# Seven block products of 256 columns in place of eight for two gates of a recurrent layer, in a fused graph stack on one core

## The chip, the cores and the metric

The kernel runs on one core of a Trainium2 chip, all in fp32. The metric is device microseconds of one execution; quoted times are medians of several executions. Engines are named as in the profile: PE (TensorE, with PEld for its weight loads), DVE (VectorE), ACT (ScalarE), POOL (GpSimd), SP (SyncE).

## The reference, cut to what matters

Four graph layers run over 128 graphs of 64 nodes with 256 features. Three are attention and relation layers, the fourth is a gated recurrence with three inner layers, and it is where the change is:

```python
def _gru_cell(inp, h, w_ih, w_hh, b_ih, b_hh):
    gi = inp @ w_ih.T + b_ih
    gh = h @ w_hh.T + b_hh
    i_r, i_z, i_n = jnp.split(gi, 3, axis=-1)
    h_r, h_z, h_n = jnp.split(gh, 3, axis=-1)
    r = jax.nn.sigmoid(i_r + h_r)
    z = jax.nn.sigmoid(i_z + h_z)
    n = jnp.tanh(i_n + r * h_n)
    return (1.0 - z) * n + z * h
...
for i in range(L):                                   # L = 3
    m = jnp.einsum('bnd,de->bne', h, weight[i])
    aggr = jnp.einsum('bst,bsd->btd', A, m)
    h = _gru_cell(aggr, h, w_ih, w_hh, b_ih, b_hh)
```

## The kernel before

16 groups of 512 rows pass through all layers. A plan interleaves the four layers of several groups on PE, so that while the recurrence of one group waits, attention matmuls of later groups fill in. The state is held transposed: `hT` and the aggregated `aT` have the 256 features in two blocks of 128 partitions and the 512 rows as columns. A "chunk" is 128 output features. For each chunk a gate of r or z is four matmuls of 512 columns (two feature blocks of `hT`, two of `aT`) into one PSUM bank:

```python
        class Gate:
            def __init__(self, name, chunk, n):
                self.pg = psum.tile([P, T], F32, name=name)          # one bank; "rz" has two, "nn" has two
            def add(self, w, m, k):
                nc.tensor.matmul(self.pg, w[:, k, self.chunk * P : (self.chunk + 1) * P], m[:, k, :], ...)

        def update(c, pr, ph, pi, pz, hT, hnew):
            nc.scalar.activation(r, pr, AF.Tanh, bias=brz[:, c : c + 1], scale=0.5)
            nc.scalar.activation(t, ph, AF.Identity, bias=bh[:, 4 + c : 5 + c])
            nc.vector.scalar_tensor_tensor(t, r, 1.0, t, op0=ALU.add, op1=ALU.mult)
            nc.vector.tensor_tensor(t, t, pi, ALU.add)
            nc.scalar.activation(nt, t, AF.Tanh, bias=bi[:, 4 + c : 5 + c])
            nc.gpsimd.tensor_tensor(d, hT[:, c, :], nt, ALU.subtract)
            yield
            nc.scalar.activation(z, pz, AF.Tanh, bias=brz[:, 2 + c : 3 + c], scale=0.5)
            nc.vector.scalar_tensor_tensor(d, z, 1.0, d, op0=ALU.add, op1=ALU.mult)
            nc.vector.scalar_tensor_tensor(hnew[:, c, :], d, 0.5, nt, op0=ALU.mult, op1=ALU.add)
        ... (allocations of the work tiles r, t, nt, z, d, two buffers each, cut)
```

`along` aggregates over the graph (matmul, then a copy of the bank into `aT`), `back` transposes the new state (PE, then a copy into `hnat`); both copies are on DVE. The eight PSUM banks are two each for "mm" and "tp" (the other layers and the helpers), "rz" and "nn".

## Time and profile before

| | before |
|---|---|
| median of 4 runs | 1657.4 us (1655.9 to 1661.9) |
| profiled span, mean granted clock of PE | 1654.2 us, 0.991 |
| PE / DVE / ACT / POOL busy | 95 / 61 / 28 / 17% |
| a steady group of 512 rows | 98.8 us |

The busy shares say which engine to look at first. The lines behind them, and PE's waits, stand in the prediction. One more reading: I split PE's time by the trace's starts of matmuls. Each record has a nominal spacing: the measured 429 ns at 512 and 216 ns at 256 columns with the line between them, and never under the 109 ns measured at 128 columns. Where a start is later than that, the doubling of a spacing in a stretch at half clock is counted as half clock, and the rest as a wait. Before, the spacings sum to 1537 us, half clock adds 7, waits are 87, and 23 us lie before the first and after the last matmul: 1654.

### The profile page before, as it was taken

How to read it: one execution, taken by the hardware profiler on the slowest of the kernel's cores; microseconds unless marked ns; L12 is line 12 of the kernel's file. 1: busy time of each engine (PE TensorE's matmuls, PEld its weight loads, DVE VectorE, ACT ScalarE, POOL GpSimd, SP SyncE). 2: the span in 40 equal slices, each digit the busy share in tenths (PEclk: the TensorE clock that was granted, in tenths of full speed). 3: DMA queues.
4: the chain of work that ended last, by engine and by line, in shares of the span. 5: the costliest groups of instructions: out<-in, count | busy, mean ns of one | idle time of the engine just before them, and what ended most of it. 6: DMA issues, size and time to landing. Idle time of an engine off the chain costs nothing.

```text
span 1654.2 us, 16189 instructions
## 1 busy us (share of the span) xinstructions
PE 1574.5 (95%) x5685; PEld 889.4 (54%) x5685; DVE 1014.3 (61%) x2403; ACT 470.9 (28%) x909; POOL 276.6 (17%) x252
## 2 busy tenths in 40 slices
PE   6898999999999999999999999999999999999997
PEld 4554555555555555556555555555555555554543
DVE  6777675757567475765757567475665656463533
ACT  3332332222222322323232232223222222222221
POOL 2111030211211111221211112111221111110110
PEclk9899999999999999999999999999999999999999
DMA  7000000100001000000100001010000000000000
GB/s 195 22 0 17 23 26 4 45 4 20 26 5 44 4 20 26 23 26 4 46 4 20 26 20 29 4 42 1 16 13 4 27 4 14 13 4 13 0 13 15
DMA packets 45890, 35.63 MB, mean 22 GB/s; under 512 B 21736, under 2 KB 44008, under 8 KB 45800
## 3 DMA queue, kind: packets, MB, share of 16 engines
q1 hardware_dynamic: 45240, 33.98, 7.3%
q8 instruction: 47, 0.77, 0.2%
q10 hardware_dynamic: 560, 0.52, 0.1%
q14 instruction: 43, 0.35, 0.1%
HBM read 25.96 MB, written 8.53 MB: 21 GB/s over the span
## 4 chain that ended last, share of the span: by engine, by line
PE 77%; DVE 14%; POOL 3%; issue 2%; ACT 2%; DMA 2%; SPq 0%; ACTq 0%; DVEq 0%; POOLq 0%
PE rz L295 33%; PE nn L295 16%; PE mm L627 6%; PE mm L231 6%; PE mm L250 4%; PE tp L264 3%; PE tp L166 3%; DVE hn L158 2%; PE tp L306 2%; DVE st L149 2%; PE mm L639 2%; DVE eb L568 1%; POOL xg L210 1%; POOL rstd L154 1%; DVE hn L209 1%
## 5 line engine op out<-in xcount | busy, mean ns | idle before, releaser
L295 PE MATMUL rz<-aT,wc 128*128 128x512 f32 x768 | 389.7, 599 | 6.7 <-DVE aT L268 6.7
L295 PE MATMUL rz<-hT,whh 128*128 128x512 f32 x768 | 386.9, 594 | 0.8 <-ACT r L317 0.8
L325 POOL TENSOR_TENSOR d<-hT,nt 128x512 f32<-128x512 f32 x96 | 124.0, 1292 | 831.6 <-ACT nt L323 824.6
L295 PEld LDWEIGHTS rz<-aT,wc 128*128 128x128 f32 x768 | 140.2, 190 | 161.2 <-issue 135.8
L295 PEld LDWEIGHTS rz<-hT,whh 128*128 128x128 f32 x768 | 135.8, 190 | 100.8 <-issue 95.1
L295 PE MATMUL nn<-aT,wc 128*128 128x512 f32 x384 | 189.4, 594 | 0.1
L295 PE MATMUL nn<-hT,whh 128*128 128x512 f32 x384 | 189.2, 593 | 0.0
L329 DVE SCALAR_TENSOR_TENSOR d<-z,d 128x512 f32<-128x512 f32 x96 | 66.1, 688 | 119.5 <-ACT z L328 68.4
L158 DVE TENSOR_SCALAR hn<-xg,mv,rstd 128x256 f32<-128x256 f32 x256 | 103.1, 447 | 43.3 <-POOL rstd L154 43.1
L149 DVE BATCH_NORM_STATS2 st<-xg 128x6 f32<-128x256 f32 x256 | 98.9, 403 | 47.3 <-POOL xg L210 41.3
L264 PEld LDWEIGHTS tp<-abd,hnat 128*128 128x128 f32 x768 | 100.4, 194 | 40.1 <-issue 30.0
L627 PE MATMUL mm<-wl,hT 128*128 128x512 f32 x248 | 119.8, 608 | 0.4 <-ACT hT L167 0.4
L317 ACT ACTIVATE r<-rz,brz 128x512 f32<-128x512 f32 x96 | 65.8, 686 | 187.9 <-PE rz L295 187.7
L166 PE MATMUL tp<-ident,hn 128*128 128x128 f32 x512 | 73.5, 281 | 45.3 <-DVE hn L158 27.4
L250 PEld LDWEIGHTS mm<-wh,eb 128*128 128x128 f32 x620 | 86.3, 191 | 55.8 <-issue 33.2
L295 PEld LDWEIGHTS nn<-aT,wc 128*128 128x128 f32 x384 | 70.9, 190 | 76.7 <-issue 72.7
L319 ACT ACTIVATE t<-nn,bh 128x512 f32<-128x512 f32 x96 | 65.8, 686 | 154.7 <-PE nn L295 154.7
L323 ACT ACTIVATE nt<-t,bi 128x512 f32<-128x512 f32 x96 | 69.2, 720 | 140.6 <-DVE t L321 102.8
L250 PE MATMUL mm<-wh,eb 128*128 128x65 f32 x620 | 100.5, 293 | 8.2 <-DVE eb L568 6.1
L328 ACT ACTIVATE z<-rz,brz 128x512 f32<-128x512 f32 x96 | 65.8, 685 | 147.7 <-PE rz L295 147.7
L264 PE MATMUL tp<-abd,hnat 128*128 128x128 f32 x768 | 102.2, 278 | 3.3 <-DVE fT L553 2.6
L166 PEld LDWEIGHTS tp<-ident,hn 128*128 128x128 f32 x512 | 60.6, 144 | 80.7 <-DVE hn L158 30.7
(161 smaller groups left out, 1822.6 us busy)
## 6 DMA issues: line engine op xcount, KB each, us to landing
out_dram<-hnat SPq DMA_DIRECT2D x16, 512.0 KB
xg<-in_x_dram SPq DMA_DIRECT2D x15, 512.0 KB
hT<-row SPq DMA_DIRECT2D x28, 256.0 KB
at<-in_adj_dram SPq DMA_DIRECT2D x64, 32.0 KB
ag<-in_adj_dram SPq DMA_DIRECT2D x16, 128.0 KB
t<-row SPq DMA_DIRECT2D x28, 64.0 KB
ihn<-in_L_gnn_w_ih_dram SPq DMA_DIRECT2D x1, 768.0 KB
hhn<-in_L_gnn_w_hh_dram SPq DMA_DIRECT2D x1, 768.0 KB
```

Of the source, the lines that this page charges most:

```text
L149: nc.vector.bn_stats(st[:, p, :], src[:, p, :])
L158: nc.vector.tensor_scalar(hn[:, p, :], src[:, p, :], mv[:, p, 0:1], rstd[:, p : p + 1], op0=ALU.subtract, op1=ALU.mult,)
L166: nc.tensor.transpose(pt[:, p * P : (p + 1) * P], hn[:, p, k * P : (k + 1) * P], ident)
L231: nc.tensor.matmul(pm[:, : D + 2 * heads], hT[:, k, p * P : (p + 1) * P], we[:, k, :], start=(k == 0), stop=(k == K - 1),)
L250: nc.tensor.matmul(pv[:, h, :], lhsT(p, h), wv[:, p, h, :], start=True, stop=True)
L264: nc.tensor.matmul(pa[:, p * P : (p + 1) * P], hnat[:, p, c * P : (c + 1) * P], abd[:, p, :], start=True, stop=True,)
L295: nc.tensor.matmul(self.pg, w[:, k, self.chunk * P : (self.chunk + 1) * P], m[:, k, :], start=(self.done == 0), stop=(self.done == self.n ...
L317: nc.scalar.activation(r, pr, AF.Tanh, bias=brz[:, c : c + 1], scale=0.5)
L323: nc.scalar.activation(nt, t, AF.Tanh, bias=bi[:, 4 + c : 5 + c])
L325: nc.gpsimd.tensor_tensor(d, hT[:, c, :], nt, ALU.subtract)
L329: nc.vector.scalar_tensor_tensor(d, z, 1.0, d, op0=ALU.add, op1=ALU.mult)
L627: nc.tensor.matmul(pm, hT[:, k, p * P : (p + 1) * P], wl[:, k, :], start=(k == 0), stop=(k == K - 1))
```

## The change

The intent: a product of a 2x2 block matrix of weights (gates r and z by two feature blocks) with a 2x2 block matrix of states (feature blocks by two halves of the rows) takes seven block products in place of eight, with sums of weights (made once), sums of states (per layer, POOL), and sums of products. Some of the latter are made by accumulating in PSUM, the others by ACT copying a running sum out of the bank and DVE adding it later. Bank "ry" takes M1, M6, M5, M3 one after the other.

```diff
+    def state_sums(m, ms, k):
+        if k == 0:
+            nc.gpsimd.tensor_tensor(ms[:, 0], m[:, 0, S1], m[:, 0, S0], ALU.subtract)
+        else:
+            nc.gpsimd.tensor_tensor(ms[:, 2], m[:, 1, S1], m[:, 0, S1], ALU.subtract)
+            nc.gpsimd.tensor_tensor(ms[:, 1], m[:, 1, S1], ms[:, 0], ALU.subtract)
+            nc.gpsimd.tensor_tensor(ms[:, 3], m[:, 1, S0], ms[:, 1], ALU.subtract)
     def recurrence(work, psum, start, src, abd, store):
         hT, aT = start
+        hS = work.tile([P, 4, T // 2], F32, name="hS")
+        aS = work.tile([P, 4, T // 2], F32, name="aS")
+        for k in range(K):
+            state_sums(hT, hS, k)
+            state_sums(aT, aS, k)
 ... (along, back: nc.vector.tensor_copy -> nc.scalar.copy for aT and hnat)
+            def mul(self, name, q, source):
+                lhsT, rhs = {
+                    1: (w[:, 0, cs], m[:, 0, S0]),
+                    2: (w[:, 1, cs], m[:, 1, S0]),
+                    3: (ws[:, 2, cs], m[:, 1, S1]),
+                    4: (w[:, 1, zs], ms[:, 3]),
+                    5: (ws[:, 0, cs], ms[:, 0]),
+                    6: (ws[:, 1, cs], ms[:, 1]),
+                    7: (w[:, 0, zs], ms[:, 2]),
+                }[q]
+                nc.tensor.matmul(ps[:, S0], lhsT, rhs, ...)
+            def r_there(self, h):
+                if h == S0:
+                    nc.vector.tensor_tensor(r, self.banks["rm"][:, S0], r, ALU.add)
+                    y = r
+                else:
+                    y = self.banks["ry"][:, S0]
+                nc.scalar.activation(r, y, AF.Tanh, bias=brz[:, self.c : self.c + 1], scale=0.5)
+                nc.vector.scalar_tensor_tensor(t, r, 1.0, t, op0=ALU.add, op1=ALU.mult)
+            def n_there(self, h):
+                nc.vector.tensor_tensor(t, t, self.banks["ni"][:, h], ALU.add)
+                nc.scalar.activation(t, t, AF.Tanh, bias=bi[:, 4 + self.c : 5 + self.c])
+                nc.gpsimd.tensor_tensor(self.d[:, h], self.hT[:, self.c, h], t, ALU.subtract)
+            def m1_there(self):   nc.scalar.copy(self.r[:, S0], self.banks["ry"][:, S0])
+            def m16_there(self):  nc.scalar.copy(self.z[:, S0], self.banks["ry"][:, S0])
+            def m165_there(self): nc.scalar.copy(self.z[:, S1], self.banks["ry"][:, S0])
+            def z_there(self, h):
+                nc.vector.tensor_tensor(z, self.banks["rz"][:, S0], z, ALU.add)
+                nc.scalar.activation(z, z, AF.Tanh, bias=brz[:, 2 + self.c : 3 + self.c], scale=0.5)
 ... (h_there: the two last steps by halves; the order of products in a layer; weight_sums)
-            turn = itertools.cycle(("mm", "tp", "rz", "nn"))
+            turn = itertools.cycle(("mt", "ry", "rm", "mt", "rz", "nh", "mt", "ni"))
-                return banks.tile(shape, dtype, name=name, tag=next(self.turn) if self.early else name)
+                tag = next(self.turn) if self.early else "mt" if name in ("mm", "tp") else name
+                return banks.tile(shape, dtype, name=name, tag=tag, bufs=3 if tag == "mt" else 1)
-                               {"hT": 3, "hnat": 2, "aT": 2, "r": 2, "t": 2, "nt": 2, "z": 2, "d": 2}))
+                               {"hT": 3, "hnat": 2, "aT": 2}))
-        start, period = 93.0, 93.0
+        start, period = 93.0, 88.0
 ... (two more numbers of the plan: 93.5 -> 88.5, 68 -> 65, recurrence work 68 -> 63)
```

S0 and S1 are the two halves of the 512 rows, and M1 to M7 the seven products, numbered in `mul`. "mm" and "tp" now share three banks; "ry", "rm", "rz", "nh" and "ni" have one each. The work tiles r, t, z, d and the new hS and aS have one buffer each. Some tiles of the preparation were also put into buffers of other tiles to make room; that is not shown here.

## The prediction

> **What bounds the kernel now.** I read the profile in this order: the page's busy shares and slices, the chain that ended last, the costliest groups, PE's waits in the middle of the run, the engines' busy time over whole groups, and two stretches of PE's order of time.
>
> ```profile
> PE 1574.5 (95%) x5685; PEld 889.4 (54%) x5685; DVE 1014.3 (61%) x2403; ACT 470.9 (28%) x909; POOL 276.6 (17%) x252
> ...
> PE   6898999999999999999999999999999999999997
> ...
> PE 77%; DVE 14%; POOL 3%; issue 2%; ACT 2%; DMA 2%; SPq 0%; ACTq 0%; DVEq 0%; POOLq 0%
> ...
> L295 PE MATMUL rz<-aT,wc 128*128 128x512 f32 x768 | 389.7, 599 | 6.7 <-DVE aT L268 6.7
> L295 PE MATMUL rz<-hT,whh 128*128 128x512 f32 x768 | 386.9, 594 | 0.8 <-ACT r L317 0.8
> ```
>
> PE is busy in nine tenths or more of almost every slice, and the matmuls that the change cuts (tile rz, gates r and z) are the costliest two groups. "Busy" alone could hide slack, since ends of matmuls are modelled, so I looked at whole groups (between stores of the output, at 1011.8, 1111.1, 1210.3 and 1308.2 us) and at what PE waits for between 190 and 1400 us:
>
> ```profile
> 1011.80:1111.10 99.30, 96.13 (x350) 53.98 (x349) 62.99 (x145) 27.89 (x53) 16.68 (x14) 1.00 0.07 19
> 1111.10:1210.30 99.20, 96.11 (x350) 54.01 (x349) 59.41 (x143) 28.35 (x53) 16.75 (x14) 1.00 0.06 18
> ```
>
> ```profile
> PE tp L166 <- DVE hnat L308: 14.3, 9, 2.1
> PE mm L250 <- DVE eb L568: 5.8, 7, 1.5
> PE rz L295 <- DVE aT L268: 5.0, 9, 0.9
> ```
>
> A group of 512 rows takes some 98.8 us, PE is idle under 3 us of it, and in 1210 us PE waits some 33 us in all. The matmuls of one group, counted at their spacing below, add up to about 98 us. So time removed from PE shows one for one, as long as no wait replaces it. The spacing is what counts, not the 594 ns of one record, which overlaps its neighbour:
>
> ```profile
> 1588.70 1.88 PE L295 MATMUL nn<-hT,whh 128*128 128x512 f32 x4
> 1590.41 1.88 PE L295 MATMUL nn<-aT,wc 128*128 128x512 f32 x4
> 1592.13 0.60 PE L306 MATMUL tp<-ident,hT 128*128 128x128 f32 x4
> ...
> 62.49 1.03 PE L609 MATMUL mm<-ihT,gT 128*128 128x256 f32 x4
> 63.36 0.49 PE L539 MATMUL mm<-dg1e,same 128*128 128x128 f32 x2
> ```
>
> Eight records of 512 columns take 3.43 us, 0.429 us each; four of 256 columns take 0.87 us, 0.217 us each. One fp32 matmul of the program is two records.
>
> **What the Trainium skill says.** "TensorE: Matmul & The Clock Gate", Back-to-back issue gap, gives N/2.4 + 2.5 ns per matmul, 216 ns at 512 columns; the trace shows twice that for each record in fp32, so the measurement is used. Its section on LDWEIGHTS gives P/1.2, 107 ns for 128 columns: eight attention records with 65 columns are spaced 0.105 us, which agrees, and a weight load therefore still fits behind a 256-column record of 0.217 us. "PSUM — Partial Sum Buffer", PSUM bank collisions raise a hardware error, says that two engines must not be in one bank at once: PE must wait until ACT or DVE has read a bank. Before, with two banks per kind, that wait is nearly absent (0.8 us on r). "SBUF — State Buffer", Who interferes with whom, says that a DVE instruction with two SBUF inputs and a POOL instruction that reads SBUF block each other. The trace is mixed: d<-z,d (two SBUF inputs) takes 688 ns and t<-t,nn (one from PSUM) 685 ns, but of two equal 1024-column steps one takes 1221 and the other 1424 ns.
>
> **The change part by part.**
> *PE.* 16 groups x 3 layers x 2 chunks = 96 chunks. Removed: 1536 records x 0.429 = 659 us. Added: 14 products x 2 records x 96 = 2688 x 0.217 = 583 us (577 if the half were exact). Saved: 76 to 82, say 78 us. In a steady group that is 4.9 of 98.8 us. Gate n, the aggregations and the layers before keep their matmuls.
> *DVE.* It loses the copies of aT (66.0) and hnat (43.8 us). Its four 512-wide steps a chunk (66.1 + 66.0 + 65.9 + 65.8 = 264 us) become eight 256-wide ones and three sums out of PSUM are added: 11 x 96 at 0.42 us (the o<-mm,rec row of 256 columns has 423 ns) = 444 us. Net +70: 1084 us, some 68% of the new time.
> *ACT.* It loses r, nt, z (65.8 + 69.2 + 65.8 = 201 us); gains six half-wide tanh (ACT's hT groups, 594 ns at 512 and 382 ns at 256 columns, give 0.83 ns a column, so 686 becomes 0.473 us, an estimate) x 96 x 0.473 = 272, three copies of 256 x 96 x 0.37 (the wh copies have 370 ns) = 107, and the aT and hnat copies, 160 x 0.583 (the wc copy of 512) = 93. Net +271: 742 us, 46%.
> *POOL.* The sums of states: eight a layer, 48 layers, 384 instructions of 256 columns. From 1292 ns at 512 and 2387 ns at 1024 columns the line gives 0.74 us at 256, an estimate: 284 us. The d steps halve and double, 192 x 0.74 = 142 instead of 124. With 16 weight sums (12 us, before the recurrence): about 590 us, 37%.
> No engine but PE comes near its limit. All three still deliver in order, and PE depends on them more: in the built program PE's waits on ACT go from 409 to 661, on DVE from 645 to 749, on POOL from 33 to 228.
> *What lands on the path.* The bank ry takes the products M1, M6, M5, M3 one after the other and ACT must copy the running sum out between them. After the last column of a product ACT starts some 0.3 us later (1642.9 to 1643.17 us for the last z), copies in 0.37, and the release costs about 0.1: 0.75 us, against 0.86 us of another product or gate placed between. It fits by 0.1 us, if ACT isn't behind a tanh that awaits DVE. The aggregation of aT is copied by ACT (0.58) and then used at once by M1; a second one is summed on POOL (0.74) before M7. In a layer without other work between I count: 0.95 us for the first aT, 0.1 before the second aggregation, 0.8 for the POOL sum of aT, 0.3 on ry: about 2.1 us. In a steady group some 10 us of other layers' matmuls lie in each recurrent layer and fill most of it; I leave 0.4 us a layer. So: 14 groups x 3 x 0.4 = 17 us, the last two groups, with little or no filler, 6 x 1.6 = 10 us, and 1 us for the start. Sum: -78 + 28 = -50, 1656 - 50 = 1606; the scheduler has placed DVE's sums well ahead of the long chains, so I take 1603.
>
> **The rivals.**
> *A. The saving passes in full.* All waits are hidden: 1656 - 78 = 1578 us, or a little under. For it: the 33 us of PE waits over 1210 us in a kernel that already has DVE and ACT between, and hnat's release (14.3 us) moves from DVE to a less busy ACT. Against it: single banks, and a tail without filler, where the whole saving of a group (5 us) is about what the waits cost.
> *B. The waits take the saving.* Single banks and POOL sums cost over 1.3 us a layer in the steady part: 42 x 1.3 + 10 = 65, so 1640 us or more. For it: DVE often has instructions of 1.2 to 1.4 us ahead of a small sum, POOL one of 2.4 us (xg, 1024 columns), and each can hold a bank or a sum back by that much. Against it: the filler of 10 us a layer, and 68% of DVE.
> *C. POOL and DVE block each other.* POOL at 37% and DVE's two-input steps at about 240 us: if 37% of 576 such steps meet a POOL instruction and wait half of 0.74 us, DVE loses 79 us, and stands at 73%. That alone is no bound; it would lengthen the waits of B. I count it as part of the high end.
> *D. The three shared banks of mm and tp* (four before) hold the other layers' matmuls back. Each bank is held for under 1.5 us and used every 1.5 to 2 us on average; I expect a few us.
>
> **Range and chances.** The floor is A's 1574 to 1578; I put one chance in ten below 1580. B with C makes 1640; one in ten above 1632. 2% faster is 1623. Prediction 1603 us, range 1580 to 1632; faster by over 2% 0.8, within 2% 0.17, slower 0.03 (it needs over 110 us of new waits).
>
> **What would show it right or wrong.** Right: r and z's matmul groups 2688 records spaced 0.217 us; a steady group of 94 to 96 us; PE's waits led by ACT copies and tanh on ry, by POOL sums on rz, by aT copies; the last group as long as before (68 us from the store at 1578.5 to that at 1646.9). DVE near 68%, ACT 46%, POOL 37%. Wrong by A: PE's waits in the middle no larger than 33 us. Wrong by B: steady groups over 97 us, with PE waiting over 1.3 us a layer; which releaser then leads tells banks from POOL sums. Wrong in the costs: a spacing of 256-column records well over 0.217 us, or POOL sums of 1 us and more.

## The result, and the profile after

| | before | after |
|---|---|---|
| median of 4 runs, us | 1657.4 | 1781.3 (1779.6 to 1786.0) |
| profiled span, clock | 1654.2, 0.991 | 1777.8, 0.966 |
| sum of matmul spacings | 1537 | 1458 |
| added by half clock | 7 | 47 |
| PE's waits | 87 | 250 |
| of these at the transposes that end a group (`back`) | 4 | 70 |
| of these at gates' matmuls | 20 | 107 |
| before the first and after the last matmul | 23 | 23 |

The ratio is 1.0747, 95% interval 1.0717 to 1.0778. The lower rows of the table are my split of the two traces. They close: -79 of spacing, +40 of half clock and +163 of waits make +124.

The page of the changed kernel, busy time by engine, PE's slices and clock, and the chain that ended last:

```profile
PE 1570.3 (88%) x6837; PEld 1132.8 (64%) x6837; DVE 1097.4 (62%) x2915; ACT 718.3 (40%) x1645; POOL 595.6 (34%) x748
...
PE   5788979899898989989898988989989898998986
...
PEclk9899999999999999999899999999999899999999
...
PE 44%; DVE 29%; POOL 14%; ACT 5%; issue 5%; DMA 2%; SPq 1%; ACTq 0%; DVEq 0%; POOLq 0%
```

PE's busy time hardly fell although 79 us of work went: busy counts records until their modelled ends, and at half clock they are longer (experiment e4 below has the same matmuls with 34 us at half clock in place of 120, and 1526.0 us of busy PE). The chain says more. PE held 77% of it before and holds 44% now; DVE (14 to 29%) and POOL (3 to 14%) took most of the rest, though neither is busy for two thirds of the span. Two whole groups, between stores of the output (columns: span, then busy time of PE, PEld, DVE, ACT, POOL, clock, DMA share, GB/s):

```profile
974.30:1081.60 107.30, 95.68 (x423) 69.06 (x422) 65.79 (x179) 44.19 (x100) 35.33 (x44) 0.98 0.07 19
1081.60:1187.70 106.10, 95.33 (x416) 68.75 (x414) 64.10 (x176) 44.61 (x100) 35.39 (x44) 0.97 0.07 18
```

These groups take 106 to 107 us in place of 99, and PE has some 11 us without work in each; before it had 3. (The steady groups take 102 to 109 us in all; and the first store comes at 245.6 us in place of 226.5, so 19 of the 124 us are lost before it.) What PE waited for over the whole run (total us, times, longest):

```profile
PE tp L324 <- DVE hT L417: 66.9, 17, 6.4
...
PE rz L363 <- DVE z L411: 18.4, 19, 2.1
PE ry L363 <- ACT z L403: 16.1, 18, 2.7
PE rz L363 <- POOL hS L295: 8.0, 4, 2.8
PE ry L363 <- ACT r L400: 6.9, 6, 1.7
```

The first line is new, and no rival had it: 16 of its 17 waits, of 3.2 to 6.4 us, stand one at each group's end, where `back` needs the last state `hT`. The others are of the kind foreseen. The end of the group stored at 1187.7 us in order of time (start, duration, engine, line, work, and in brackets the idle time before and its releaser):

```profile
1177.56 0.73 POOL L293 TENSOR_TENSOR hS<-hT 128x256 f32<-128x256 f32 x1 [8.57 <-PE rz L363]
1177.62 1.11 ACT L396 ACTIVATE t<-t,bi 128x256 f32<-128x256 f32 x2 [1.37 <-DVE t L395]
...
1178.94 0.74 POOL L296 TENSOR_TENSOR hS<-hT,hS 128x256 f32<-128x256 f32 x1
...
1180.99 0.74 POOL L397 TENSOR_TENSOR d<-hT,t 128x256 f32<-128x256 f32 x1
...
1183.03 0.74 POOL L397 TENSOR_TENSOR d<-hT,t 128x256 f32<-128x256 f32 x1
...
1183.80 1.26 DVE L416 SCALAR_TENSOR_TENSOR d<-z,d 128x256 f32<-128x256 f32 x2 [5.29 <-POOL d L397]
...
1185.79 1.11 PE L324 MATMUL tp<-ident,hT 128*128 128x128 f32 x4 [4.44 <-DVE hT L417]
```

Read it upwards. PE stood 4.44 us for the last hT; DVE stood 5.29 us for d; POOL made d at 1180.99 and 1183.03, although its input, the last tanh of ACT, was there at 1178.7. Between lie state sums of the *next* group, each of some 0.74 us: of its eight first sums, five stand ahead of the first d in POOL's order and seven ahead of the second. They had not run earlier because hS has one buffer, and the first of them had to wait (8.57 us of idle POOL) for PE to have read hS for the last time in this group. A lightly loaded engine thus becomes a bottleneck for 5 us by what stands ahead in its queue. Before, the same place had no gap.

The gap has a sequel. Busy time and clock of the stretches after it in the changed kernel, and of the same place in the kernel before:

```profile
1183.00:1190.00 7.00, 4.21 (x20) 4.21 (x21) 3.23 (x7) 1.28 (x2) 1.45 (x3) 0.53 0.20 65
```

```profile
1204.00:1211.00 7.00, 7.00 (x37) 4.51 (x36) 3.20 (x7) 1.66 (x3) 0.31 (x1) 1.00 0.01 4
```

At 0.53 PE runs at half clock. In the trace, PE spends 120 us at half clock after the change and 28 us before, mostly in pieces of 3.4 or 6.8 us that follow a gap. The Trainium skill describes this on "TensorE: Matmul & The Clock Gate", What's actually happening: an idle window of about 3.4 us throttles the array, and a busy one releases it. This trace agrees on the length of a piece (3.41 us), but not that the whole window must be idle: here half clock began at 1183.4 us, 2.0 us after PE fell idle. It cost 40 us more than before, which the prediction had not counted at all.

### The profile page after: what moved, and what is told of

It reads as the page before. It is cut to its first block, busy times and chain, and to the rows that moved or that the text cites. A ratio compares the mean times of both kernels' runs of the same rounds, so it can differ in the third digit from the quotient of the medians.

```text
span 1777.8 us, 20195 instructions
## 1 busy us (share of the span) xinstructions
PE 1570.3 (88%) x6837; PEld 1132.8 (64%) x6837; DVE 1097.4 (62%) x2915; ACT 718.3 (40%) x1645; POOL 595.6 (34%) x748
## 4 chain that ended last, share of the span: by engine, by line
PE 44%; DVE 29%; POOL 14%; ACT 5%; issue 5%; DMA 2%; SPq 1%; ACTq 0%; DVEq 0%; POOLq 0%
PE ry L363 9%; PE mm L234 5%; PE ni L376 4%; PE nh L376 4%; PE mm L253 4%; POOL d L397 4%; PE rz L363 4%; DVE hn L161 3%; PE mm L743 3%; DVE st L152 3%; DVE d L416 3%; DVE hT L417 3%; PE tp L267 3%; POOL rstd L157 3%; POOL xg L213 2%
## 5 line engine op out<-in xcount | busy, mean ns | idle before, releaser
L397 POOL TENSOR_TENSOR d<-hT,t 128x256 f32<-128x256 f32 x192 | 146.1, 768 | 504.6 <-ACT t L396 504.4
L376 PE MATMUL nh<-hT,whh 128*128 128x512 f32 x384 | 202.1, 609 | 0.7 <-ACT t L380 0.4
L376 PE MATMUL ni<-aT,wc 128*128 128x512 f32 x384 | 196.8, 595 | 0.0
L412 ACT ACTIVATE z<-z,brz 128x256 f32<-128x256 f32 x192 | 97.2, 506 | 156.9 <-DVE z L411 156.6
L416 DVE SCALAR_TENSOR_TENSOR d<-z,d 128x256 f32<-128x256 f32 x192 | 90.5, 489 | 112.0 <-POOL d L397 106.2
L396 ACT ACTIVATE t<-t,bi 128x256 f32<-128x256 f32 x192 | 93.3, 503 | 126.4 <-DVE t L395 123.7
L363 PE MATMUL rz<-hS,whh 128*128 128x256 f32 x384 | 120.3, 395 | 26.7 <-DVE z L411 18.4
L363 PE MATMUL ry<-hS,wsum 128*128 128x256 f32 x384 | 119.3, 392 | 23.5 <-ACT z L403 16.1
L363 PE MATMUL rz<-aS,wc 128*128 128x256 f32 x384 | 115.8, 383 | 3.2 <-POOL aS L295 3.0
L363 PE MATMUL ry<-aS,wsum 128*128 128x256 f32 x384 | 114.9, 381 | 0.0
```

The source lines that it names most:

```text
L363: nc.tensor.matmul(ps[:, S0], lhsT, rhs, start=new, stop=(source == 1 and q in (2, 3, 4)), skip_group_check=True)
L376: nc.tensor.matmul(ps, w[:, k, f : f + P], m[:, k, :], start=new, stop=not new)
L396: nc.scalar.activation(t, t, AF.Tanh, bias=bi[:, 4 + self.c : 5 + self.c])
L397: nc.gpsimd.tensor_tensor(self.d[:, h], self.hT[:, self.c, h], t, ALU.subtract)
L412: nc.scalar.activation(z, z, AF.Tanh, bias=brz[:, 2 + self.c : 3 + self.c], scale=0.5)
L416: nc.vector.scalar_tensor_tensor(d, self.z[:, h], 1.0, d, op0=ALU.add, op1=ALU.mult)
```

## The experiments

Each number is to be read against 1781 (changed) and 1657 to 1660 (before, in the same rounds). "Wrong" marks kernels whose result is wrong. All eighteen were timed in three rounds beside the kernel before. The batches ran on different chips, and the kernel before took 1656.8 to 1660.3 us in them: a difference of a few us between batches says nothing.

| experiment | us | ratio to before, 95% | clock |
|---|---|---|---|
| e2 last d on DVE | 1720.0 | 1.0359, 1.0329 to 1.0389 | 0.984 |
| e3 no copies out of ry (wrong) | 1743.8 | 1.0503, 1.0465 to 1.0540 | 0.961 |
| e4 no state sums (wrong) | 1660.5 | 1.0008, 0.9980 to 1.0037 | 0.990 |
| e5 before, three helper banks | 1661.8 | 1.0018, 0.9987 to 1.0049 | 0.991 |
| e6 sums after the last d | 1724.3 | 1.0401, 1.0365 to 1.0437 | 0.982 |
| e7 = e6, two ry banks | 1750.8 | 1.0564, 1.0546 to 1.0581 | 0.975 |
| e8 = e7, chunks interleaved | 1778.8 | 1.0742, 1.0717 to 1.0767 | 0.969 |
| e13 room made, nothing else | 1780.2 | 1.0735, 1.0707 to 1.0762 | 0.968 |
| e12 r, t, z, d doubled | 1777.4 | 1.0714, 1.0684 to 1.0743 | 0.963 |
| e14 = e12 with e6 | 1714.6 | 1.0358, 1.0324 to 1.0393 | 0.984 |
| e9 = e4 with e3 (wrong) | 1647.1 | 0.9936, 0.9920 to 0.9953 | 0.984 |
| e10 first sums early, doubled | 1727.6 | 1.0414, 1.0390 to 1.0439 | 0.980 |
| e11 = e9, no reads of rm, rz (wrong) | 1649.8 | 0.9951, 0.9930 to 0.9972 | 0.984 |
| e15 old plan | 1794.1 | 1.0799, 1.0769 to 1.0829 | 0.952 |
| e16 before, aT and hnat copies on ACT | 1643.5 | 0.9905, 0.9888 to 0.9921 | 0.987 |
| e17 = e11, no DVE sums (wrong) | 1634.7 | 0.9843, 0.9825 to 0.9861 | 0.983 |
| e18 = e16, es and fT on ACT | 1618.3 | 0.9751, 0.9732 to 0.9769 | 0.992 |
| e19 = e10, es and fT on ACT | 1743.5 | 1.0499, 1.0471 to 1.0527 | 0.966 |

### First batch: which part costs

Theory: POOL's order at the group ends, then reads between products (rival B). Rivals: the three helper banks (D), DVE and POOL blocking each other (C).

**e2**, the last d of a group on DVE, off POOL's queue:

```diff
-                nc.gpsimd.tensor_tensor(self.d[:, h], ...)
+                engine = nc.vector if self.c == 1 and self.i == LAYERS - 1 else nc.gpsimd
+                engine.tensor_tensor(self.d[:, h], ...)
```

> The changed kernel with one edit: in the third layer's second chunk the subtraction h - n runs on DVE in place of POOL, so POOL's eight sums for the next group cannot stand in front of it. Theory 1 (at a group's end POOL's queue holds back the last h): the 69.7 us that PE waits for the new h before the last transposes, 16 times some 4.2 us, fall to under 20 us, half-clock time falls from 120 us to under 90 us, and the kernel takes some 1700 us (1685 to 1725). Theory 2 (single banks that are read in mid-accumulation are the main cost): those waits only show elsewhere, time 1760 us or more. Theory 3 (POOL is too slow for the sums wherever they stand): POOL sums then hold the next group's first products, time 1740 us or more, with PE waiting for hS and aS over 40 us.

61 us came back, PE's wait for the last hT fell from 67 to 31 us and half-clock time from 120 to 56 us. The place is right; the gap did not close.

**e3**, the three copies of running sums read h, of the same size, and not the bank (wrong result):

```diff
-                nc.scalar.copy(self.r[:, S0], self.banks["ry"][:, S0])
+                nc.scalar.copy(self.r[:, S0], self.hT[:, self.c, S0])
 ... (the same for the two copies into z)
```

> The changed kernel with a wrong result on purpose: ACT's three copies a chunk read h from SBUF in place of the bank ry, so nothing reads ry in mid-accumulation; the number of instructions and their engines stay. Theory 2 (mid-accumulation reads): PE's waits on ACT for ry (some 41 us) go, and with what follows from them the time falls by 40 to 70 us, to 1710 to 1740 us, while the waits for the last h stay near 70 us. Theory 1: those waits only, so under 45 us gained, and the last h still costs about 70 us.

38 us came back. ACT's releases at ry are gone from PE's waits; waits for DVE at other layers' tiles rose from 46 to 61 us.

**e4**, no state sums; M4 to M7 read h and a directly (wrong result):

```diff
     def state_sums(m, ms, k):
-        ... (four POOL subtractions)
+        pass
-                    4: (w[:, 1, zs], ms[:, 3]),
+                    4: (w[:, 1, zs], m[:, 1, S0]),
 ... (5, 6, 7 likewise)
```

> The changed kernel with a wrong result on purpose: no sums of states on POOL at all (384 instructions fewer, some 295 us of POOL), the products read unsummed slices instead. Theory 1: the last-h wait goes (-65 us), the direct waits on POOL (-13 us) and part of the clock's loss (-15 us): some 1690 us (1670 to 1710). Theory 2: 1740 us or more. If it is well under 1670 us, the sums cost more than the waits on PE show.

121 us, nearly the whole loss. But 1660 is level with the kernel before, some 80 us above the 1578 us that the kernel before would take less the matmuls saved: without any state sum, gates' matmuls still wait 96 us.

**e5**, the kernel before with "mm" and "tp" in three shared banks:

```diff
-            turn = itertools.cycle(("mm", "tp", "rz", "nn"))
+            turn = itertools.cycle(("mt", "rz", "nn", "mt", "rz", "nn", "mt"))
 ... ("mt" for mm and tp, with three buffers)
```

> The kernel before with one edit: the helper tiles mm and tp share three banks, as after the change, in place of two each; gates keep theirs. If the new division of the helper banks costs by itself, this is slower by over 10 us; I expect within 5 us of 1656 us, since waits of other layers' matmuls are the same in both budgets (about 48 us on DVE).

No difference: the interval holds 1. Rival D falls, as far as the kernel before can show it; three banks against four in the changed kernel were not tried.

### Second batch: mending the order, then the banks

**e6**, only POOL's order changed: the first sums of a group are issued after the last d of the group before.

```diff
-        for k in range(K):
-            state_sums(hT, hS, k)
-            state_sums(aT, aS, k)
+        with tc.issue_after(LAST[-1].ins) if LAST else ExitStack():
+            for k in range(K):
+                state_sums(hT, hS, k)
+                state_sums(aT, aS, k)
 ... (LAST collects POOL's subtractions d)
```

> The changed kernel with nothing moved or removed but one order: POOL's eight first sums of a group are placed behind the last subtraction h - n of the group before, in POOL's queue only, without a wait. If the order in POOL's queue is the cause at the groups' ends, PE's wait for the last h falls from 69.7 us to under 15 us, half-clock time from 120 us to under 60 us, and the time from 1781 us to 1680 to 1700 us, better than 1720 us (the subtraction on DVE). If POOL's work itself is too much there, the wait moves to the next group's first products (rz waiting for hS or aS, over 40 us) and the time stays above 1720 us.

57 us came back, less than expected; `back` still waits 29 us:

```profile
PE tp L327 <- DVE hT L420: 29.0, 17, 3.2
```

The same place in this kernel, in order of time, shows why:

```profile
1147.62 1.80 DVE L419 SCALAR_TENSOR_TENSOR d<-z,d 128x256 f32<-128x256 f32 x2 [1.13 <-POOL d L400]
...
1148.22 0.91 POOL L293 TENSOR_TENSOR aS<-aT 128x256 f32<-128x256 f32 x1
1149.10 0.90 POOL L295 TENSOR_TENSOR hS<-hT 128x256 f32<-128x256 f32 x1
1149.34 1.80 DVE L420 SCALAR_TENSOR_TENSOR hT<-d,t 128x256 f32<-128x256 f32 x2
```

Two DVE steps with both inputs in SBUF take 1.80 us, where two such steps alone take about 0.86 (e4's d has 431 ns each), and POOL's sums beside them take 0.90 in place of 0.73. The two take turns; that is rival C's block, at the one place where it lies on the path. Over the whole run it shows in the mean of DVE's d, here for the changed kernel and then for e4 (busy us, mean ns, idle before and its releasers):

```profile
L416 DVE SCALAR_TENSOR_TENSOR d<-z,d 128x256 f32<-128x256 f32 x192 | 90.5, 489 | 112.0 <-POOL d L397 106.2 <-ACT z L412 5.7
```

```profile
L410 DVE SCALAR_TENSOR_TENSOR d<-z,d 128x256 f32<-128x256 f32 x192 | 79.4, 431 | 63.2 <-POOL d L391 56.7 <-ACT z L406 6.4
```

58 ns a step; with hT (504 against 465) that is 19 us of DVE, and over all of DVE's 2915 instructions 39 us (1097.4 against 1058.1 of busy time), not the 79 us that the prediction allowed for.

**e7** is e6 with two banks for ry, at the price of two in place of three for the helpers; **e8** is e7 with the products of the two chunks interleaved, so that two other products or gates lie between a readout of ry and the next product into the same bank, in place of one.

```diff
-            turn = itertools.cycle(("mt", "ry", "rm", "mt", "rz", "nh", "mt", "ni"))
+            turn = itertools.cycle(("mt", "ry", "rm", "mt", "rz", "nh", "ry", "ni"))
-... bufs=3 if tag == "mt" else 1)
+... bufs=2 if tag in ("mt", "ry") else 1)
```

> As the run before it, and the bank ry is doubled at the cost of one helper bank (two in place of three), with the order of products as it was. Only the second chunk's first product can gain (about 10 us of waits on the tanh of r); with two helper banks other layers may wait more. I expect within 15 us of the run before, 1675 to 1705 us.

```diff
             yield b.both("rm", 2)
+            yield b.both("ry", 1)
+            b.m1_there()
             yield a.both("ry", 5)
             a.m165_there()
             a.z_there(S1)
             yield b.gate("nh", 0)
+            yield b.both("ry", 6)
+            b.m16_there()
             yield a.both("ry", 3)
 ... (the same for the rest of chunk b)
```

> As the run before it, with the products of the two chunks interleaved so that two products lie between a readout of ry and the next product into the same bank, in place of one. If the single bank with one product between is what PE waits for (ACT's copies 31 us, tanh of r 10 us, DVE's sum of z 23 us), these 64 us fall below 30 us, and the time comes to 1620 to 1650 us, below the kernel before (1656 us). If the waits come from ACT's and DVE's own queues, whatever the distance, it stays at 1670 us or more.

Both missed by far, in the wrong direction. e7 lost 26 us against e6: one bank less for the helpers costs more than a second ry gives, though the two are not separated. In e8 PE waited 43 us for ACT's copy of M1 alone. More distance between products on ry did not help in this form. But the trace shows that e8 was no clean test of it: that copy itself stood for the one tile r, which a DVE step still had to read (in e7 this wait is 3.4 us):

```profile
ACT r L403 <- DVE t L394: 40.6, 56, 2.1
```

e8 with two buffers of r was not run, so the theory of too short a distance stays untested.

### Third batch: single work tiles, and adding up

Among ACT's long waits in the changed kernel is one of 82 us for the state of the chunk before: with one buffer of t, the copy of nh into t stands until the last hT step is done, and ACT's copies out of ry stand behind it. Theory S made this the cause of the gates' waits. Doubling the tiles needs room, so a control came with it.

```diff
-            xg = work.tile([P, G, D], F32, name="xg", bufs=6)      # e13, e12, e14
+            xg = work.tile([P, G, D], F32, name="xg", bufs=5)
-            at = work.tile([P, G // 2, 2, N], I32, name="at", bufs=3)
+            at = work.tile([P, G // 2, 2, N], I32, name="at", bufs=2)
-                               {"hT": 3, "hnat": 2, "aT": 2}))      # e12, e14
+                               {"hT": 3, "hnat": 2, "aT": 2, "r": 2, "t": 2, "z": 2, "d": 2}))
```

> Control for the next two runs: the changed kernel with five buffers of xg in place of six and two of the adjacency in place of three, to make room. Loads are issued long ahead, so every theory expects no difference: 1781 us within 8. If it is slower than 1790, the room itself costs and the next two are read against this run and not against the changed kernel.

> The changed kernel with the room of the control and the work tiles r, t, z and d doubled again, as they were before the change. Theory S (single work tiles: the copy of nh into t waits for the last step on hT of the chunk before, ACT works in order, so the copies out of the bank ry stand behind it): ACT's wait in t for DVE's hT falls from 82 us to under 15, PE's waits for ACT and DVE on r and z fall from about 70 us to under 35, time 1715 to 1745. Theory B (one bank ry read four times a chunk is itself the cause): ACT's wait falls but PE's waits on r and z stay at 60 us or more, time 1765 to 1785. The gaps at group ends (70 us of back) stay under both.

> Doubled r, t, z, d together with the first state sums of a group held back behind the last d steps of the group before. The order alone gave 1724. If the two causes are separate they add: 1724 less 40 to 55, so 1670 to 1685 and about level with the kernel before. If the doubled tiles help only where the order of POOL was already in the way, 1715 to 1725. If theory B holds, 1715 to 1725 too, with PE's waits on z at 50 us or more.

The control is at 1780 as expected. e12 is at 1777, no different from the control. ACT's wait in t for hT (82 us in the changed kernel's row of t) left the list of waits, as planned, yet PE's own waits in the steady part, between 200 and 1500 us, are as they were (first the changed kernel, then e12):

```profile
PE tp L324 <- DVE hT L417: 49.7, 12, 6.4
PE rz L363 <- DVE z L411: 16.4, 17, 2.1
PE ry L363 <- ACT z L403: 13.3, 13, 2.7
```

```profile
PE tp L324 <- DVE hT L417: 50.7, 12, 6.5
PE rz L363 <- DVE z L411: 15.1, 18, 1.9
PE ry L363 <- ACT z L403: 12.2, 10, 2.6
```

Theory S falls: 82 us of waits of an engine that is not the bottleneck cost nothing. e14, at 1715, cannot be told from e6 at 1724 (the intervals overlap).

**e9** joins e4 and e3 (wrong result):

> Wrong result on purpose: no state sums and the three copies out of the bank ry replaced by copies of h of the same size. Without sums alone the time was 1660, without these reads alone 38 us less than the changed kernel. If the two add, 1620. If the reads only hurt because the sums kept DVE and POOL busy, 1650 to 1660 as without sums. Waits that remain then belong to the sums of rm and rz on DVE and to the single work tiles, since PE no longer waits for any copy between products: expected 100 to 120 us of PE waits, against 164 without sums alone.

1647: only 13 us less than without sums alone, where 38 would have come by adding. PE's waits at gates fell from 96 to 54 us, and its waits elsewhere rose from 68 to 91. The wait moves on to the next thing that is late.

### Fourth batch: what is still late

**e10**, first sums made well before the recurrence, into doubled hS and aS (with the control's room):

```diff
     def before_recurrence(work, psum, src, adjacency, abd):
 ...
+        hS = work.tile([P, 4, T // 2], F32, name="hS")
+        aS = work.tile([P, 4, T // 2], F32, name="aS")
+        for k in range(K):
+            state_sums(hT, hS, k)
+            state_sums(aT, aS, k)
         yield -1.5
-        return hT, aT
+        return hT, aT, hS, aS
```

> The changed kernel with the eight first sums of a group made before its recurrence starts, into doubled tiles, so that they stand neither before nor beside the last steps of the group before. Theory P (place of the sums at the group end): PE's wait in the transposes at group ends falls from 70 to under 10 us, the half-clock time from 120 to under 50 us, time 1685 to 1705, below the 1715 to 1724 of the runs that only held the sums back. Theory L (load of POOL beside DVE at all times): the gap goes but other waits grow, 1710 to 1730.

The gap at group ends is closed: PE's wait for the last hT is 5 us in place of 67. But the time is 1728, as theory L had it, because the gates' waits rose from 107 to 131 us. What PE waited for over the run:

```profile
PE ry L363 <- ACT z L403: 25.9, 23, 3.7
...
PE rz L363 <- DVE z L411: 24.4, 19, 2.6
...
PE rm L363 <- DVE r L386: 10.1, 7, 3.7
...
PE tp L324 <- DVE hT L417: 5.4, 4, 3.2
```

So of the 121 us of the state sums some 54 to 61 (e2, e6, e10) are their place at the group ends, and the other 60 or so are there wherever they stand. Whether as load of POOL beside DVE, or because products must wait for the sums (PE's direct waits for POOL at gates are 12 us in the changed kernel), no run separates.

**e11** takes the last reads between products away: DVE's sums read h and not rm and rz (wrong result):

```diff
-                    nc.vector.tensor_tensor(r, self.banks["rm"][:, S0], r, ALU.add)
+                    nc.vector.tensor_tensor(r, self.hT[:, self.c, h], r, ALU.add)
-                nc.vector.tensor_tensor(z, self.banks["rz"][:, S0], z, ALU.add)
+                nc.vector.tensor_tensor(z, self.hT[:, self.c, h], z, ALU.add)
```

> Wrong result on purpose: as the run without sums and without copies out of ry (1647 us), and DVE's three sums a chunk read h in place of the banks rm and rz, at the same size. No product then waits for a partial sum to be read, except M3's reader. Theory R (release of rm and rz by DVE): its 22 us of PE waits go, and with them part of the waits of the other layers, 1610 to 1630. Rival (DVE is simply late with its many small steps, so PE waits for it somewhere else): 1640 to 1650, with PE's waits for DVE at other layers' tiles at 65 us or more.

1650, no gain: what the rival forecast. PE no longer waits for DVE's z at all, and waits elsewhere for DVE in its place, at an attention tile and at the states (whole run):

```profile
PE mm L253 <- DVE eb L676: 22.9, 12, 2.7
...
PE tp L318 <- DVE hT L411: 15.1, 18, 2.7
```

**e17** leaves DVE's three sums a chunk out altogether (wrong result):

```diff
-                    nc.vector.tensor_tensor(r, self.hT[:, self.c, h], r, ALU.add)
-                nc.vector.tensor_tensor(z, self.hT[:, self.c, h], z, ALU.add)
```

> Wrong result on purpose: as the run whose DVE sums read h in place of the banks (1650 us), but those three DVE sums of 256 columns a chunk are left out altogether: 288 steps of 0.42 us, 120 us of DVE, of which the chains to tanh also get shorter. Theory V (DVE in order is late): PE's waits for DVE, 86 us at other layers, fall to under 65, time 1615 to 1635. If DVE's load isn't it, 1643 to 1652.

1635: 15 us of time for 92 us less of DVE's busy time (1071 in e11, 979 here, by their pages). The time fell to the upper edge of what theory V expected, but the test set for the waits was not met: PE's waits for DVE away from the gates, 83 us in e11's trace, are 81 here (63 at other layers' tiles and 18 at the transposes of the state). The two traces can't say where the 15 us went: e11's fastest execution was profiled and e17's slowest, and their spans differ by 3 us (1642.4 and 1639.6). V is partly right at most.

**e15** puts the plan's four numbers back, **e16** moves only the copies of aT and hnat in the kernel before:

```diff
-        start, period = 93.0, 88.0                     # e15, and the three others likewise
+        start, period = 93.0, 93.0
-        nc.vector.tensor_copy(aT[:, c, :], pa)         # e16, and hnat likewise
+        nc.scalar.copy(aT[:, c, :], pa)
```

> The changed kernel with the four numbers of the plan as before the change (a period of 93 in place of 88, the other layers placed for 93.5 and 68). If the tighter plan is no part of the loss, 1775 to 1790. If it starves the recurrence of filler or crowds it, a change of over 15 us, most likely to 1750 to 1765.

> The kernel before with only the copies of aT and hnat moved from DVE to ACT. The copies take about as long there (0.58 us against some 0.7), and ACT is less busy: 1650 to 1662 if the move costs nothing. If ACT's order (tanh steps that wait for DVE) holds the aggregation back, over 1665.

The tighter plan is no part of the loss: without it the kernel is, if anything, slower (13 us by the medians; the intervals just touch). And the move of copies to ACT, taken alone, is a gain of 17 us in the kernel before (1643.5).

**e18** and **e19** go further that way, with the small copies es and fT on ACT too, in e16 and in e10:

```diff
-            nc.vector.tensor_copy(es[:, p, :], pm[:, D : D + 2 * heads])
+            nc.scalar.copy(es[:, p, :], pm[:, D : D + 2 * heads])
-                nc.vector.tensor_copy(fT, pt[:nh, :P])
+                nc.scalar.copy(fT, pt[:nh, :P])
```

> The kernel before with the aT and hnat copies on ACT (1643.5 us alone) and also the small copies es and fT on ACT, where DVE waited 132 us for ACT's wh copy of the same bank. DVE loses 28 us of work and most of that wait. Theory V: 1630 to 1642. If the small waits that are left don't end on the path, 1640 to 1648. It should beat both kernels either way.

> The changed kernel with early first sums in doubled tiles (1727.6 us alone), and es and fT on ACT. Theory V: 1705 to 1720, since DVE no longer waits 78 us for ACT's wh. If ACT's longer queue holds the copies out of bank ry back, 1728 or more. It stays above the kernel before in any case.

e18 is correct and beats both kernels: 1618 us, 2.5% under the kernel before, more than expected. Its page, one group's worth of its steady part (the columns as above), and PE's waits between 200 and 1500 us, of which only 9.4 us are left:

```profile
PE 1566.8 (97%) x5685; PEld 890.0 (55%) x5685; DVE 892.4 (55%) x2087; ACT 572.3 (35%) x1225; POOL 277.8 (17%) x252
```

```profile
1100.00:1200.00 100.00, 99.30 (x358) 55.62 (x358) 55.05 (x131) 37.23 (x77) 18.88 (x16) 1.00 0.04 13
```

```profile
PE mm L250 <- DVE eb L568: 5.7, 6, 1.6
PE mm L250 <- DVE o L253: 2.0, 1, 2.0
```

In e16, DVE stood 132 us for ACT's wh copy before it could copy es out of the same bank; with both on ACT, that wait is gone. In the changed kernel (e19) the same edit costs 16 us: ACT has es and fT in its order beside the copies out of ry, PE's waits at ry for the copies into z rose from 37 to 44 us, and half-clock time from 70 to 119.

## Why the prediction was wrong, by its own steps

- **PE's saving** of 76 to 82 us was right: the sum of spacings fell by 79, and 256-column records are spaced 216 ns. One reading beside it was off: a group's matmuls add up to 94 us by their spacings before, not 98.
- **The engines' loads** were right: DVE 1084 predicted and 1097 measured, ACT 742 and 718, POOL 590 and 596; a POOL sum 0.74 and 0.74 to 0.80 us, a half tanh 0.473 and 0.47 to 0.51. DVE's is in part luck: the 1084 held nothing for blocking by POOL, which is in the 1097; without the state sums (e4) DVE has 1058. The counts of waits in the built program (409 to 661 and so on) stand in no run.
- **What lands on the path** is the step that failed. It said 0.4 us a layer in 14 groups, 1.6 in the last six layers and 1 at the start, 28 us. Measured: 163 us more of waits and 40 of half clock. By time, 19 us were lost up to the first store, and the last group took 72.6 us, not 68. By cause, these terms make it up.
  - *Group ends*, 66 us more of waits, were not in the sum. The prediction took POOL's load for what counts ("No engine but PE comes near its limit") and did not read the order of POOL's queue against the buffers: with a single hS, next group's sums can only run at this group's end, ahead of d. e2, e6 and e10 show that the place costs 54 to 61 us, with the half clock that follows it.
  - *Gates' waits*, 87 us more than before, are 1.8 us for each of 48 layers. The 0.4 rested on "some 10 us of other layers' matmuls" filling the waits; but the order of PE's instructions is fixed in the program, and filler placed elsewhere does not move into a wait (argued; no run moved filler alone). Rival B had 1.3 us a layer and named the right kind.
  - *Half clock*, 40 us more, was not in the sum.
  - The other 10 us are waits at other layers' tiles.
- **Rival C** was sized too large (39 us of DVE, 19 of them in d and hT, against 79), but it was also taken as only lengthening waits; at the ends of groups it kept most of 29 us open after the order was mended (e6).
- **Rival D**, a few us expected: nothing in the kernel before (e5).
- **The chance of slower**, 0.03, was justified by "it needs over 110 us of new waits". They came, because the terms all add, and two of them, the group ends and the half clock, had not been weighed at all.
- Moving the aT and hnat copies was put down as load on ACT only; alone, in the kernel before, it is worth 17 us of the time (e16). If it were worth as much in the changed kernel, which no run shows and e19 makes doubtful, the rest of the change would have lost some 138 us, not 124.

Shown by runs: the state sums account for 121 us, about half of it by place; the copies out of ry for 38 us with the sums and 13 without; the reads out of rm and rz for nothing by themselves; DVE's extra sums for 15. Open: e17, with all that removed, is at 1635, and 1578 was the floor. Its PE waits 138 us, 63 of it for DVE at other layers' tiles and 18 for DVE at the transposes of the state, against 87, 48 and 3 in the kernel before. That DVE, now with small half-width steps in a fixed order, is late for those layers is argued from these waits and from e16 and e18; no run settles it, since e17's trace does not show them lower. For e8's worse order the trace points to the one tile r; how it would do with two is open.

## What to carry to other kernels

Before trusting a saving of 5% on the bottleneck engine, read for every single-buffered tile that the change adds which instruction of the next round writes it first, what that waits for, and what stands behind it in its engine's queue: an engine at a third of its load can hold the path by order alone. Removing one wait at a time tends to hand it to the next late producer, so a row of kernels that adds removals up says more than any single one. Lightening the late producer (here 23 us of small copies taken off DVE after 99 us of large ones) did what seven products in place of eight did not.

## What the Trainium skill lacked or had wrong

- "TensorE: Matmul & The Clock Gate" (HAM oscillation, and the table of what matters for kernels) speaks of idle gaps over about 3 us; where it speaks of shorter idling that throttles, it gives no length. Here pieces of 3.4 us at half clock also followed single gaps of 1.8 to 2.7 us (at 319.8, 1040.0, 1268.7 and 1377.9 us of the changed kernel; gaps 1.8, 2.2, 2.3 and 2.7 us). In the 3.4 us before each piece PE was idle for no longer than that one gap.
- The same page's gap of N/2.4 + 2.5 ns has no word on fp32. The passes of true fp32 do stand on "FP8 and Floating Point Precision", TensorE Precision Notes, but not how they show in a trace: here as two records a matmul, each 429 ns at 512 and 216 ns at 256 columns, so four times the page's gap for the product.
- "SBUF — State Buffer" states the block between DVE and POOL as one side waiting for the whole instruction; it gives no cost when both issue in a row. Here they took turns: 0.90 us a step on both sides for 256 columns, against 0.43 on DVE and 0.73 on POOL alone.
